# Sums of squares in four quarters of the array, and a square root taken by sides

## The chip, the core and the metric

The kernel runs on one core of a Trainium2 chip. The metric is the device time of one execution in microseconds (us); the median of the runs stands for a kernel. Engines are named as in the profile: PE (TensorE, matrix products), PEld (its weight loads), DVE (VectorE), ACT (ScalarE), POOL (GpSimd) and SP (SyncE, which here issues DMAs).

## The reference, cut to what matters

Four layers follow one another on a 48-channel image of 128 x 128: an attention over all pixels, sweeps along rows and columns, a convolution with 8 x 8 patches, and a state-space scan. Only the beginning of the first is edited:

```python
qkv = jnp.einsum('bchw,oc->bohw', x, qkv_w)
qkv = jax.lax.conv_general_dilated(qkv, dw_w, window_strides=(1, 1), padding='SAME',
                                   feature_group_count=3 * c, ...)
q, k, v = jnp.split(qkv, 3, axis=1)
...
def _l2norm(t, eps=1e-12):
    n = jnp.sqrt(jnp.sum(t * t, axis=-1, keepdims=True))
    return t / jnp.maximum(n, eps)
q = _l2norm(q)
k = _l2norm(k)
attn = jax.nn.softmax(jnp.einsum('bnc,bmc->bnm', q, k) * temperature, axis=-1)
```

Each pixel is a token with 48 channels of q, k and v. The token's q and its k are divided by their lengths, so the kernel needs, for every token, a sum of squares over the 48 channels of q and another over those of k.

## The kernel before, in words

`tile_kernel` (L1779) runs `attention`, `sweeps`, `patch_conv`, `scan_stats` and `scan` one after the other. `attention` (L121) has a first stage, which makes q, k and v, and then `attend` (L424), which does the softmax.

The first stage goes over 8 bands of 16 image rows, and each band has two *takes* of 8 rows, t0 to t15; a take is 1024 tokens, as two halves of CH = 512. Everything is fp32.

- `band(b)` (L237) fills one of two band buffers and one of two `rest` buffers: DVE writes normalised rows (L94), then 15 DMAs on SP's queue copy shifted rows (L265, L268 and twelve at L277) for the convolution. Band b+1 is filled while band b is worked on.
- `conv` (L280) does the 1x1 and 3x3 convolution as products on PE. `p[0]` and `p[1]` (one per half, a PSUM bank each) hold q and k: the 48 channels of q with their padding on partitions 0 to 63, those of k on 64 to 127. `pv` holds v of both halves, one on partitions 0 to 63, one on 64 to 127. The last products, `pv<-rest`, have 48 rows and 64 columns each: the first in rows 0 to 47 and columns 0 to 63 of the array, the second in rows 64 to 111 and columns 64 to 127.
- `take` (L319) squares `p[0]` and `p[1]` on ACT into `sq`, copies `pv` to `vt` on ACT, and sums the squares over the channels with one 128x128 product per half: `blk` is block diagonal, with ones in its two blocks of 48 x 64. So the result `pss[n]` has on partitions 0 to 63, in every row, the sum over q, and on 64 to 127 that over k. ACT takes the square root into `nrm`. PE then transposes `vt` into `pt`.
- `scale` (L346), on DVE: reciprocal of `nrm` (`rn`), and `f` = `p` times `rn`. DVE also copies `pt` into `v` (L378), after which POOL sets a part of `v` to one (L379).
- `split` (L353) of take k is issued after take k+1: ACT rounds `f` into the first part of `hl`, POOL subtracts for the second (L362), and per half four DMAs on SP carry `hl` off to `qm` and `keys` (L363 to L366). There are two `hl` buffers, one per half, so the casts of take k wait for the DMAs of take k-1.
- `moving(0)` (L162) loads the first queries back, with 12 DMAs on SP. It is issued in band 4, ahead of the DMAs of band 5.

The order on ACT and PE is that of the program (`InOrder`). The queues of all engines, SP's too, run in order: an instruction that waits holds up those behind it. A take on ACT is: two squares, `vt`, two roots, then the two casts of the split of the take before. In the last take the two `p` are copied to `late`, which frees their banks for `attend`.

`patch_conv` holds another place that matters below: its products `f<-qkv,fm` are four 64x64 products with 384 columns, one in each quarter of the array, written to two banks, one for the upper row half and one for the lower. Its source line in the profile, like that of all recorded engines, is L49.

Of the kernel before, what the change touches and what calls it, by code (L numbers as in the profile page):

```python
# [22 lines left out]
AF = mybir.ActivationFunctionType  # L23
# [97 lines left out]
def attention(ctx, tc, x1, mp, const, ins):  # L121
# [4 lines left out]
    ident, blk = const["ident"], const["blk"]  # L126
# [6 lines left out]
    for i in range(HALF // PART):  # L133
        t = images.tile([128, PART], F32, name=f"x{i}")
        nc.gpsimd.memset(t[32:64], 0.0)
        for half in range(2):
            at = half * HALF + i * PART
# [39 lines left out]
    with ExitStack() as a:  # L177
        act, pe = InOrder(tc, nc.scalar), InOrder(tc, nc.tensor)
# [140 lines left out]
        def take(t0, p, pv):  # L319

            sqs, psss, nrms = [], [], []
            for n in range(2):
                sqs.append(sp.tile([128, CH], F32, name="sq"))
                act.activation(sqs[n], p[n], AF.Square)
            vt = once.tile([128, CH], F32, name="vt")
            act.copy(vt, pv)

            for n in range(2):
                psss.append(ps2.tile([128, CH], F32, name="pss"))
                pe.matmul(psss[n], lhsT=blk, rhs=sqs[n], start=True, stop=True)  # L330
                nrms.append(rp.tile([128, CH], F32, name="nrm"))
                act.activation(nrms[n], psss[n], AF.Sqrt)
            if t0 == N - 2 * CH:

                for n in range(2):
                    act.copy(late[n], p[n])
                p = late
            pt = ps1.tile([128, 4, 2, 64], F32, name="pt")
            for i in range(4):
                pe.transpose(  # L340
                    pt[:, i].rearrange("t n c -> t (n c)"), vt[:, i * 128 : (i + 1) * 128], ident
                )
            tv = slice(t0 // 128, t0 // 128 + 8)
            own = {}

            def scale(get):  # L346
                for n in range(2):
                    rn = rnp.tile([128, CH], F32, name="rn")
                    nc.vector.reciprocal(rn, nrms[n])
                    own[n] = get("f", n)  # L350
                    nc.vector.scalar_tensor_tensor(own[n], rn, 1e12, p[n], ALU.min, ALU.mult)

            def split(act, get):  # L353

                r, at = divmod(t0, N // 4)
                r *= 32
                for n in range(2):
                    f, hl = own[n], get("hl", n)
                    to = slice(t0 + n * CH, t0 + (n + 1) * CH)
                    kc = slice(at + n * CH, at + (n + 1) * CH)  # L360
                    act.copy(hl[:, 0].bitcast(F32R), f)
                    nc.gpsimd.tensor_sub(hl[:, 1].bitcast(F32R), f, hl[:, 0])  # L362
                    nc.sync.dma_start(parts_of[:, :, to], hl[0:C])  # L363
                    nc.sync.dma_start(keys[r : r + 32, 0:2, kc].bitcast(F32), hl[64:96])
                    for i in range(2):
                        nc.sync.dma_start(  # L366
                            keys[r + 16 * i : r + 16 * i + 16, 2, kc].bitcast(F32),
                            hl[96 : 64 + C, i],
                        )

            def get(name, n):
                if name == "hl":
                    return hlp.tile([128, 2, CH], F32, name=name)
                return fp.tile([128, CH], F32, name=name)

            if p is not late:
                scale(get)
            nc.vector.tensor_copy(v[:, tv, :].rearrange("t (n i) c -> t i n c", n=2), pt)  # L378
            nc.gpsimd.memset(v[:, tv, C:64], 1.0)  # L379
            return scale, split, get  # L380
# [3 lines left out]
        for b in range(NB):  # L384
            if b == NB // 2:
                first = moving(0)
            nxt = band(b + 1) if b + 1 < NB else None
            for y in range(0, R, 8):
                p = [ps.tile([128, CH], F32, name="p") for _ in range(2)]
                pv = ps1.tile([128, CH], F32, name="pv")  # L390
                t0 = (b * R + y) * W
                conv(p, pv, cur, y)
                more = take(t0, p, pv)
                if last:
                    last[1](act, last[2])
                last = more
            cur = nxt
# [1604 lines left out]
```

## Time and profile before

| what | us |
|---|---|
| median of 3 runs (lowest to highest) | 7003.15 (6998.90 to 7007.36) |
| the profiled execution | 7006.47 |
| its span, first to last instruction | 7004.7 |
| PE busy | 5671.9 (81% of the span) |
| ACT busy | 4517.3 (64%) |
| DVE busy | 4462.8 (64%) |
| POOL busy | 2825.9 (40%) |

The takes lie between 43 and 247 us of the span, `attend` from there to 3380 us. The busy shares are averages over stages with different bounds; a stage is read by its own rows, and by what ends last in it. In the profile a product of fp32 shows as two matrix passes, so two products count as x4. "rn", "pss" and so on are the tiles' names without buffer numbers, and `128*64 128x512` is the size of the weights, and that of the moving operand.

### The profile page before, as it was taken

The numbers are of one execution on the slowest core, as the hardware profiler recorded it, in microseconds if no ns is written. First come the engines' busy times: TensorE is split into PE (matmuls) and PEld (weight loads), VectorE is DVE, ScalarE is ACT, GpSimd is POOL, SyncE is SP. The second block draws the span as 40 slices with busy tenths as digits, with TensorE's granted clock in tenths as the row PEclk, the third lists the DMA queues.
The fourth block names the chain that finished last, engine by engine and source line by source line (L and its number), as shares of the span: only waits on it lengthen the run. The fifth ranks groups of instructions, "written<-read, shape, count | busy, mean of one in ns | idle before, by whom it ended". The sixth has DMA issues, their size and how long they took to land.

```text
span 7004.7 us, 217413 instructions
## 1 busy us (share of the span) xinstructions
PE 5671.9 (81%) x97896; PEld 3328.3 (48%) x97896; DVE 4462.8 (64%) x4604; ACT 4517.3 (64%) x6731; POOL 2825.9 (40%) x623
## 2 busy tenths in 40 slices
PE   8999999999999999999999996555455545555555
PEld 3444444444444444444677653444443434344444
DVE  6444434444344443444445445999999999999998
ACT  2677777777777777777440134766666666666665
POOL 2100000000000000000102223999999999999998
PEclk9999999999999999999999997777666767776666
DMA  5200000000000000000100112565566656566665
GB/s 101 65 11 16 16 17 12 15 16 16 17 11 17 16 16 17 11 16 10 34 21 3 46 23 63 161 165 165 161 160 159 164 159 162 155 166 167 182 177 147
DMA packets 214187, 534.76 MB, mean 76 GB/s; under 512 B 44419, under 2 KB 76210, under 8 KB 211346
## 3 DMA queue, kind: packets, MB, share of 16 engines
q1 hardware_dynamic: 201623, 511.07, 27.5%
q8 instruction: 769, 12.60, 0.8%
q10 hardware_dynamic: 11627, 9.71, 0.6%
q14 instruction: 168, 1.38, 0.1%
HBM read 464.51 MB, written 28.31 MB: 70 GB/s over the span
## 4 chain that ended last, share of the span: by engine, by line
PE 60%; DVE 25%; issue 6%; POOL 4%; ACT 2%; DMA 2%; SPq 1%; ACTq 0%; DVEq 0%; POOLq 0%
PE s L49 45%; DVE h L1754 22%; PE p L49 7%; PE y L49 3%; POOL h L49 3%; PE pp L49 1%; DVE xb L49 1%; PE pc L49 1%; ACT dA L49 1%; PE pv L49 1%; PE po L49 1%; DMA du<-rep 1%; DVE y L49 0%; ACT L49 0%; POOL y L1148 0%
## 5 line engine op out<-in xcount | busy, mean ns | idle before, releaser
L49 POOL TENSOR_TENSOR h<-du,bt 128x3072 f32<-128x3072 f32 (+1 forms) x386 | 2560.1, 6674 | 100.0 <-DMA du<-rep 56.0
L49 ACT ACTIVATE x<-s,temp 128x512 f32<-128x512 f32 x3076 | 1832.3, 693 | 677.7 <-PE s L49 677.7
L1754 DVE TENSOR_TENSOR_SCAN h<-dA,carry,h 128x1024 f32<-128x1024 f32 x864 | 1939.8, 2324 | 34.4 <-ACT dA L49 30.8
L49 PE MATMUL s<-x,v 128*64 128x512 f32 x8192 | 1870.5, 598 | 0.0
L49 ACT ACTIVATE dA<-dt,a 128x1024 f32<-128x1024 f32 x1152 | 1287.3, 1118 | 853.9 <-DVE h L1754 843.2
L49 PE MATMUL y<-h,cw 128*32 128x48 f32 x49152 | 908.0, 247 | 929.4 <-issue 478.6
L49 PE MATMUL s<-mq,keys 32*128 32x512 f32 x20480 | 1337.7, 401 | 2.4 <-ACT late L49 1.3
L49 PEld LDWEIGHTS y<-h,cw 128*32 128x32 f32 x49152 | 817.2, 141 | 1050.3 <-issue 626.6
L819 POOL MEMSET xb<- 128x256 f32 (+1 forms) x2 | 0.8, 412 | 3116.2 <-DVE end L49 3116.2
L49 PEld LDWEIGHTS s<-mq,keys 32*128 32x128 f32 x20480 | 952.5, 183 | 578.6 <-issue 415.2
L49 DVE TENSOR_TENSOR both<-s,both 128x512 f32<-128x512 f32 x480 | 331.9, 691 | 1350.6 <-PE s L49 1350.6
L49 PEld LDWEIGHTS s<-x,v 128*64 128x64 f32 x8192 | 542.8, 136 | 1064.6 <-issue 877.8
L49 DVE COPY x<-s 128x512 f32<-128x512 f32 x1020 | 704.0, 690 | 418.0 <-PE s L49 406.6
L49 ACT ACTIVATE x<-x,temp 128x512 f32<-128x512 f32 x1020 | 693.2, 749 | 0.0
L1754 DVE TENSOR_TENSOR_SCAN h<-dA,h 128x1024 f32<-128x1024 f32 x288 | 635.3, 2269 | 36.0 <-ACT dA L49 26.4
L49 PE MATMUL yz<-ev,sel 128*8 128x48 f32 x4096 | 192.5, 260 | 266.4 <-ACT ev L49 265.0
L49 PEld LDWEIGHTS yz<-ev,sel 128*8 128x8 f32 x4096 | 162.2, 106 | 324.7 <-ACT ev L49 296.2
L49 PE MATMUL p<-xb,l_w 112*48 112x78 f32 (+8 forms) x6096 | 227.3, 223 | 18.7 <-DVE xb L49 7.4
L49 PE MATMUL p<-xa,l_w 112*48 112x78 f32 (+8 forms) x6096 | 227.5, 224 | 15.1 <-DVE xa L49 6.0
L49 PEld LDWEIGHTS p<-xb,l_w 112*48 112x48 f32 x6096 | 193.4, 123 | 52.6 <-DVE xb L49 36.3
L49 PEld LDWEIGHTS p<-xa,l_w 112*48 112x48 f32 x6096 | 193.9, 123 | 48.7 <-DVE xa L49 30.5
L941 POOL TENSOR_TENSOR xb<-xb,xa 48x2048 f32<-48x2048 f32 (+2 forms) x10 | 45.1, 4506 | 402.4 <-DVE xa L49 371.5
(210 smaller groups left out, 3422.8 us busy)
## 6 DMA issues: line engine op xcount, KB each, us to landing
du<-rep SPq DMA_DIRECT2D x768, 256.0 KB
dt<-rep SPq DMA_DIRECT2D x768, 256.0 KB
mq<-qm SPq DMA_DIRECT2D x128, 128.0 KB
mq<-qm SPq DMA_DIRECT2D x256, 64.0 KB
qm<-hl SPq DMA_DIRECT2D x30, 192.0 KB
rep<-dd SPq DMA_DIRECT2D x24, 192.0 KB
yd<-ys ACTq DMA_DIRECT2D x256, 12.0 KB
keys<-hl SPq DMA_DIRECT2D x30, 128.0 KB
```

What stands on the lines that cost most here:

```text
L49: ins = method(*args, **kwargs).ins
L819: nc.gpsimd.memset(b[:, lines, pad], 0.0)
L941: nc.gpsimd.tensor_add(xr, xr, u[0:C, x : x + xr.shape[2], E : E + H].rearrange("c w h -> c h w"),)
L1754: nc.vector.tensor_tensor_scan(h[:, p, k, :], dA, h[:, p, k, :], carry[:, i, k : k + 1] if ci else 0.0, ALU.mult, ALU.add,)
```

## The change

The one product per half becomes two products of 64 rows and 64 columns, one for q's squares and one for k's. For the first half they lie in the two diagonal quarters of the array; for the second half in the other two, so that q's sums land on partitions 64 to 127 of `pss[1]` and k's on 0 to 63. All four are issued before the first square root. The root of the first half stays one activation; that of the second half becomes two, one for each side, which put the sides back.

```diff
+            sides = [slice(0, 64), slice(64, 128)]
             for n in range(2):
                 psss.append(ps2.tile([128, CH], F32, name="pss"))
-                pe.matmul(psss[n], lhsT=blk, rhs=sqs[n], start=True, stop=True)
+                for side in range(2):
+                    at = sides[side]
+                    pe.matmul(
+                        psss[n][sides[side ^ n]],
+                        lhsT=blk[at, at],
+                        rhs=sqs[n][at],
+                        start=True,
+                        stop=True,
+                    )
+            for n in range(2):
                 nrms.append(rp.tile([128, CH], F32, name="nrm"))
-                act.activation(nrms[n], psss[n], AF.Sqrt)
+                if n == 0:
+                    act.activation(nrms[n], psss[n], AF.Sqrt)
+                    continue
+                for side in range(2):
+                    act.activation(nrms[n][sides[side]], psss[n][sides[1 - side]], AF.Sqrt)
```

## The prediction

> **What bounds the kernel now.** I read the stretches by stage first, to see which engine fills the stage that is edited (columns: stretch, its length, then busy time and count of PE, PEld, DVE, ACT, POOL, granted clock, DMA share, GB/s).
>
> ```profile
> 43.00:247.00 204.00, 201.27 (x640) 75.32 (x640) 140.78 (x93) 61.88 (x110) 38.62 (x45) 0.98 0.46 98
> 247.00:3380.00 3133.00, 3131.45 (x28650) 1493.59 (x28652) 1269.89 (x1818) 2454.78 (x4099) 5.22 (x5) 1.00 0.05 15
> ```
>
> The sixteen takes (8 rows of the image each, t0 to t15) fill 43 to 247 us and TensorE is busy in 201 of 204. The attention after them is filled by TensorE too, so an earlier end of the takes moves everything behind it. A busy PE says little by itself; the chain of waits, cut to this stage, says it is the bound (start, length, what).
>
> ```profile
> 70.39 6.21 PE p L49 x16
> ...
> 177.19 1.98 DMA keys<-hl
> ...
> 180.57 3.00 PE pss L49 x4
> ```
>
> One take repeats every 12.29 us (p starts at 57.93, 70.22, 82.52, 94.81 in the timeline). Once, before t10's products, the chain leaves PE and runs through SP's queue and a DMA. The stage so has two bounds: PE, and at one place SP.
>
> Then PE's timeline, around one take's products and in the later patch stage:
>
> ```profile
> 66.96 1.07 PE L49 MATMUL pv<-rest,wt 48*64 48x512 f32 x4
> 67.97 1.98 PE L49 MATMUL pss<-sq,blk 128*128 128x512 f32 x4
> 68.50 0.19 PEld L49 LDWEIGHTS pss<-sq,blk 128*128 128x128 f32 x1 [0.24 <-issue]
> 68.93 0.19 PEld L49 LDWEIGHTS pss<-sq,blk 128*128 128x128 f32 x1 [0.24 <-issue]
> 69.79 0.60 PE L49 MATMUL pt<-ident,vt 128*128 128x128 f32 x4
> ...
> 3944.31 0.88 PE L49 MATMUL f<-qkv,fm 64*64 64x384 f32 x8
> 3945.11 0.87 PE L49 MATMUL po<-k,gm 128*64 128x384 f32 x4
> ```
>
> Each product is two passes (x4 for two products), 0.43 apart, one behind the other: from 67.97 to 69.79, 1.82 us. `f` is the row that decides: four 64x64 products in the four quarters, eight passes of 384 columns, done in 0.80. A 384-column pass is 0.43 x 384/512 = 0.32; two are 0.64, four would be 1.29. So four quarters do run abreast here. `pv<-rest` has two diagonal quarters: four passes in 1.01, not 1.72.
>
> **The change part by part.** *Products.* Removed per take: four full passes, 1.72. Added: eight quarter passes, four abreast, 0.86. The first pass after a change of tile size costs about 0.1 more than 0.43 (67.97 to 68.50 is 0.53), and the load ahead of it can't be prefetched (about 0.1). Before, that falls between `pv<-rest` (64-wide quarters) and pss (whole array); after, pss has the quarters of `pv<-rest` and the switch falls between pss and the transposes. One switch either way. Start of `pv<-rest` to the next take's p: now 70.22 - 66.96 = 3.26; then 0.91 + 0.96 + 0.53 = 2.40. Saved 0.86 per take. The transposes also wait for vt on ACT (68.17 + 0.58 = 68.75); they would start at 68.83, so it just fits (0.05 a take if it doesn't).
>
> Here a rule of the Trainium skill speaks against the change: TensorEngine Tiling, Restrictions and Gotchas, Gotcha 1, says that different row tiles cannot access one PSUM bank simultaneously. In `f` each row half has its own bank; in the new code each pss bank is written by both row halves. By the rule the first product's two quarters go one behind the other, and so do the second's; in order of issue only the middle two of the four overlap: six passes, 2.6 us, 0.86 more per take instead of less. But `pv<-rest` is two row halves into the one bank of pv, and takes 1.01, as `p<-rest` does with two banks (63.18 to 64.24, 1.06). The row contradicts the rule for two quarters; no row shows it for four. I take abreast (sum -10.3), and keep the rule (sum +11) for the rivals.
>
> *Square roots.* The second is split: one activation more per take, 0.49 from start to start (245.75 to 246.24 below), whether on 64 or 128 partitions (the copy on 64x512 is 578 ns, that on 128x512 585). 16 x 0.49 = 7.8 us on ACT, which is busy 62 of 204. The 5 us ACT waits for PE's p in most takes cover it. Without that cover it would cost 0.49 a take; that happens once, at the end.
>
> ```profile
> 245.75 0.60 ACT L49 ACTIVATE nrm<-pss 128x512 f32<-128x512 f32 x1 [0.26 <-PE pss L49]
> 246.24 1.07 ACT L49 COPY late<-p 128x512 f32<-128x512 f32 x2
> ```
>
> t15's copies `late` release the banks of the attention. After: products done at 244.65, roots at 244.70, 245.18, 245.66, `late` at 246.15 instead of 246.24. t15 gains 0.1, not 0.86. Reading PSUM partitions 64 to 127 into 0 to 63 on ACT is not in the trace; DVE does it in `second`. I take no cost.
>
> *Order.* No DVE or POOL instruction changes place; PE and ACT only have the new ones. On SP one 16-row DMA to `keys` of t0's split comes two places earlier, ahead of one to `qm` and one to `keys`; it needs less than these, and SP is idle there until 72.47: nothing. The product that waits for the second square is now the third; that square is done at 65.48, over 2 us before (t10 apart, below).
>
> *What is late next.* DVE needs 2 x (3.35 + 0.68) + 0.63 + about 1 = 9.7 per take; PE's new period is 11.43, so it stays ahead. SP does not:
>
> ```profile
> 153.86 0.58 SPq L168 DMA_DIRECT2D mq<-qm  x1
> ...
> 159.68 0.52 SPq L265 DMA_DIRECT2D band<-band  x1
> 160.25 3.41 SPq L268 DMA_DIRECT2D band<-band  x2
> 163.71 8.64 SPq L277 DMA_DIRECT2D rest<-band  x12
> ...
> 176.56 1.22 SPq L366 DMA_DIRECT2D keys<-hl  x2
> ```
>
> Band 5 and t7's split stand behind the 12 DMAs of `moving(0)` (5.8 us). t8's casts to hl on ACT wait for t7's buffers (until 179.40), and t10's squares wait behind those casts: pss of t10 starts at 180.57, 1.9 late. From band 3 (104.73) to 177.78 SP has only two real gaps: 2.8 before t4's split (124.40) and 2.1 before t6's (148.99). Both end with POOL's subtraction, queued behind a memset that follows the copy of the take's pt; so their ends come with PE. A take's first root comes 0.2 earlier within the take. Band 3 itself so comes 3 x 0.86 + 0.2 = 2.8 earlier (t2's split before it hangs on t3's copy), t4's split 5 x 0.86 + 0.2 = 4.5, t6's 7 x 0.86 + 0.2 = 6.2. Each gap loses 1.7 and is left with 1.1 and 0.4; from t6's split on SP is dense, nothing more can be won, and t10's squares come 6.2 earlier. PE gets there 10 x 0.86 + 0.1 = 8.7 earlier. So 2.5 of the gain turns into stall: 1.9 becomes 4.4.
>
> The Trainium skill (TensorE: Matmul & The Clock Gate, Part 1) has the clock halved after an idle window of about 3.4 us. In the trace 1.9 idle was enough: granted clock 0.50 from 182 to 184, and pss to p took 3.64 instead of 2.26, a loss of 1.4. By the rule the longer stall costs one window at half, 1.7. I take 1.5, as now; none would give 1.2 more, two windows 1.7 less.
>
> Sum: up to t10's pss 6.2; that block itself 0.6 (two passes saved, but the second pair waits 0.5 for the second square); t11 to t14 4 x 0.86 = 3.4; t15 0.1. Together 10.3. The profiled execution took 7006.5 (span 7004.7, 1.8 around it) and would take 6996.2; it stands 3.3 above the median, within 6998.9 to 7007.4. From the median: 7003.15 - 10.3 = 6992.9.
>
> **The rivals.** *Less stall.* If SP issues some 4% quicker (`rest` in 7.8, not 8.6) and the clock stays up, 13; without any stall 15 x 0.86 + 0.1 + 3.4 = 16.4: 6987 to 6990. For it: the other bands' take 7.7 to 7.8, one 8.5. Against: SP is dense, and 5% slower over the 100 us of its dense stretch it gives back 5: 6998.
>
> *Two abreast.* Two quarters, then two: four passes again, PE as now, 0.5 more on ACT at the end: 7003.5. Against it, `f`.
>
> *The bank serialises (slower).* Place: the pss block. Price: the rule's six passes, +0.86 a take, 13.8, less some 3 of the stall it hides: +11, 7014; all eight one behind another, 3.43 instead of 1.72, 27.4 - 3 = +24, 7027. It decides from a block over 1.82 us. For it: four abreast in shared banks is in no row. Against: `pv<-rest`.
>
> **How the numbers follow.** A measurement of this kernel can tell about 0.2%, 14 us, from no change. As drawn up, 0.53, of which a tenth reads beyond 14; less stall 0.25, most of it beyond 14 once the scatter of 4 either way is added; two abreast 0.10; serialised 0.12, mostly over. Faster 0.27, same 0.62, slower 0.11. The likeliest's own range, 6989 to 6998, is the clock's (-1.2 to +1.7), SP's 5, and the scatter of 4. The range that holds 8 in 10 takes in less stall with its scatter and two abreast, and leaves out the serialised case: 6984 to 7004.
>
> **What would show it.** pss as x8 with 64*64, `pv<-rest` to pss 0.91, pss to pt 0.96; p every 11.43; t10's pss at about 174.4 after 4.4 idle behind `sq`; ACT's late copies near 236. A pss block of 1.8 or more, a take not shorter than 12.29, or transposes waiting for vt by more than 0.1 would prove it wrong; t10 without a longer stall would move it to 6988.

## The result, and the profile after

| | before | after |
|---|---|---|
| median of 22 runs each (lowest to highest) | 7002.97 (6996.47 to 7010.94) | 6993.90 (6984.93 to 6996.71) |
| the profiled execution | 7006.47 | 6985.35 |
| its span | 7004.7 | 6983.5 |
| first p of t1 to the attention's first product | 57.93 to 247.41 = 189.48 | 54.36 to 234.57 = 180.21 |

The ratio is 0.9985 with a 95% interval of 0.9979 to 0.9991: 9.1 us less, a small gain, within the 0.2% that was called no change. 6992.9 was forecast.

The two profiled executions differ by 21 us, and that is not the size of the change. From t1's first p to the attention the difference is 9.3; t0, which that stretch leaves out, saves another 0.9. So 10.2 come from the edited stage. The rest lies outside it: t0's products started 1.6 earlier in this execution (41.22 against 42.86), its p then took 1.0 less (7.07 against 8.09), as the granted clock left 0.50 sooner, and the stages from the attention's first product on were some 8 shorter. A second execution of the same kernel (the seventh experiment) took as long as before for those later stages (6757.5 from the attention's first product to the end of the span, before 6757.3), so these 8 are scatter and not the change.

The stage in the stretches (stretch, its length, busy time and count of PE, PEld, DVE, ACT, POOL, granted clock, DMA share, GB/s):

```profile
43.00:237.00 194.00, 187.97 (x735) 69.70 (x737) 144.68 (x96) 74.33 (x129) 40.71 (x47) 0.98 0.48 103
237.00:3370.00 3133.00, 3131.95 (x28646) 1470.90 (x28642) 1268.60 (x1818) 2455.80 (x4101) 3.13 (x3) 1.00 0.06 15
```

PE is still what fills it, with 188 of 194; ACT went from 62 to 74, of which 16 more roots are some 10; the attention is as it was. The chain of waits of this execution does not reach back into the takes (its first piece is at 234.47), so a take's order is read from PE's timeline (start, length, what):

```profile
63.39 0.65 PE L49 MATMUL pv<-rest,wt 48*64 48x512 f32 x2
63.42 0.65 PE L49 MATMUL pss<-sq,blk 64*64 64x512 f32 x2
63.87 0.60 PE L49 MATMUL pv<-rest,wt 48*64 48x512 f32 x2
63.90 1.43 PE L49 MATMUL pss<-sq,blk 64*64 64x512 f32 x6
65.26 0.66 PE L49 MATMUL pt<-ident,vt 128*128 128x128 f32 x4
65.75 5.32 PE L49 MATMUL p<-band,wt 128*128 128x512 f32 x12
...
159.31 7.09 PE L49 MATMUL p<-band,wt 128*128 128x512 f32 x12 [2.28 <-DMA band<-band]
170.11 1.08 PE L49 MATMUL pv<-rest,wt 48*64 48x512 f32 x4
172.48 1.56 PE L49 MATMUL pss<-sq,blk 64*64 64x512 f32 x8 [1.29 <-ACT sq L49]
174.46 5.32 PE L49 MATMUL p<-band,wt 128*128 128x512 f32 x12
...
218.93 1.20 PE L49 MATMUL pss<-sq,blk 64*64 64x512 f32 x8
220.06 0.65 PE L49 MATMUL pt<-ident,vt 128*128 128x128 f32 x4
```

The first six lines are one take. From `pv<-rest` to the transposes it takes 1.87, where 0.91 + 0.96 was forecast; one p follows another every 11.39 (before 12.29, forecast 11.43). But the four quarters do not start together: two passes of pss start 0.03 after `pv<-rest`, beside it. The middle lines are t10 with its stall, now two waits (2.28 and 1.29), neither of which is the 4.4 that was forecast. The last two, in t14, are the four quarters abreast in two banks: eight passes in 1.13, where two by two they would need four times 0.43. From `pv<-rest` (218.19) to the transposes this take needs the same 1.87; why it goes the other way is open.

ACT's timeline, around one take's roots and at the end of the stage:

```profile
64.59 0.58 ACT L49 COPY vt<-pv 128x512 f32<-128x512 f32 x1 [2.68 <-PE pss L49]
65.38 1.81 ACT L49 ACTIVATE nrm<-pss 128x512 f32<-128x512 f32 x3 [0.20 <-PE pss L49]
...
231.57 1.81 ACT L49 ACTIVATE nrm<-pss 128x512 f32<-128x512 f32 x3 [0.22 <-PE pss L49]
233.39 1.07 ACT L49 COPY late<-p 128x512 f32<-128x512 f32 x2
```

By the order of the program the first half's two products are issued first. Yet the first half's root waits 0.20 and starts at 65.38, when the *last* passes are done (the row of six ends at 63.90 + 1.43 = 65.33). So the pair that ran beside `pv<-rest` isn't the first half's, though that is issued first: it is the second half's, in the quarters that `pv<-rest` leaves free. And three roots take 1.81; with 0.60 for one, that is 0.605 from one to the next and not 0.49. Reading the other side's partitions cost nothing that shows: a root by sides took 0.591, and one on its own side (experiment 6) as long.

### The profile page after: what moved, and what is told of

Same layout as the page of the kernel before. It is cut to its first block, busy times and chain, and to the rows that moved or that the text cites. A ratio compares the mean times of both kernels' runs of the same rounds, so it can differ in the third digit from the quotient of the medians.

```text
span 6983.5 us, 217558 instructions
## 1 busy us (share of the span) xinstructions
PE 5650.6 (81%) x97960; PEld 3297.6 (47%) x97960; DVE 4464.2 (64%) x4604; ACT 4528.4 (65%) x6747; POOL 2826.0 (40%) x623
## 4 chain that ended last, share of the span: by engine, by line
PE 56%; DVE 25%; issue 6%; POOL 4%; ACT 2%; DMA 1%; SPq 0%; ACTq 0%; DVEq 0%; POOLq 0%
PE s L49 45%; DVE h L1768 23%; PE p L49 6%; POOL h L49 3%; PE y L49 3%; PE pp L49 1%; PE pc L49 1%; DVE xb L49 1%; ACT dA L49 1%; PE po L49 1%; DMA du<-rep 1%; DVE y L49 1%; ACT L49 0%; POOL y L1162 0%; POOL y L1163 0%
## 5 line engine op out<-in xcount | busy, mean ns | idle before, releaser
L49 PEld LDWEIGHTS s<-mq,keys 32*128 32x128 f32 x20480 | 930.2, 183 | 599.2 <-issue 415.6
L49 PE MATMUL p<-xa,l_w 112*48 112x78 f32 (+7 forms) x6096 | 228.7, 224 | 14.9 <-DVE xa L49 5.9
```

The lines of the kernel that those rows point to most:

```text
L49: ins = method(*args, **kwargs).ins
```

## The experiments

Each is compared with the kernel before on its own chip. "Stage" is the time from t1's first p to the attention's first product. "Lost" is what the takes from t1 to t15 took beyond 14 times their ordinary period.

| kernel | ratio (95% interval) | period | lost | stage |
|---|---|---|---|---|
| before | 1 | 12.29 | 3.6 | 189.5 |
| after | 0.9985 (0.9979 to 0.9991) | 11.39 | 6.7 | 180.2 |
| 1 both halves on the diagonal | 0.9997 (0.9988 to 1.0006) | 12.25 | 2.0 | 187.0 |
| 2 both off the diagonal | 0.9993 (0.9984 to 1.0002) | 11.40 | 7.5 | 181.6 |
| 3 after, queries loaded in band 7 | 0.9980 (0.9971 to 0.9989) | 11.39 | 0 | 173.5 |
| 4 before, queries loaded in band 7 | 0.9997 (0.9988 to 1.0006) | 12.29 | 0 | 185.8 |
| 5 halves swapped, queries in band 7 | 0.9976 (0.9966 to 0.9987) | 11.39 | 0 | 173.3 |
| 7 after once more | 0.9981 (0.9972 to 0.9990) | 11.39 | 8.1 | 181.6 |
| 8 halves swapped | 0.9981 (0.9972 to 0.9990) | 11.39 | 8.7 | 181.8 |
| 9 as 5, once more | 0.9975 (0.9966 to 0.9985) | 11.39 | 0 | 173.2 |

The theory after the first result: the gain comes from the quarters that `pv<-rest` leaves free; a part of it is lost, at t10 above all, to SP's queue. The rivals: smaller products are quicker wherever they lie; the four run abreast and that is the gain; the stall at t10 has nothing to do with SP's order.

**1, both halves on the diagonal.** The products keep their new size and lie where `pv<-rest` lies; both roots stay whole.

```diff
-                        psss[n][sides[side ^ n]],
+                        psss[n][sides[side]],
```

> Both halves' products in the two diagonal quarters, each root one activation again (128 partitions). Two theories of where the 0.9 us per take comes from. Free quarters: it comes from the pair in the off-diagonal quarters, which runs beside pv<-rest (itself on the diagonal); without such a pair the passes queue up behind pv<-rest as two and two: start of pv<-rest to pt 2.73 us instead of 1.87, a take 12.25 to 12.29 apart, time that of the kernel before (ratio 0.9995 to 1.0005). Smaller products: it comes from products of 64x64 being cheaper in themselves: 1.87 as in the changed kernel, ratio 0.9985.

Its timeline of PE:

```profile
88.25 1.08 PE L49 MATMUL pv<-rest,wt 48*64 48x512 f32 x4
89.16 1.88 PE L49 MATMUL pss<-sq,blk 64*64 64x512 f32 x8
90.98 0.66 PE L49 MATMUL pt<-ident,vt 128*128 128x128 f32 x4
```

No pss pass starts until `pv<-rest` is through, and the eight passes take 1.82, two by two: what the four full ones took. The median is 6996.56 against 6996.84 before. So neither the product's size nor its instruction count gains anything; of 0.90 per take, 0.86 are gone. It also shows the "two abreast" rival at its price. Its stage is 2.5 shorter than before all the same: 0.6 is the takes' 0.04, and most of the rest is that the clock was not halved at t10 in this execution.

**2, both halves off the diagonal.** All four products now lie in the two free quarters, and both roots go by sides.

```diff
-                        psss[n][sides[side ^ n]],
+                        psss[n][sides[1 - side]],
...
-                if n == 0:
-                    act.activation(nrms[n], psss[n], AF.Sqrt)
-                    continue
```

> Both halves' products in the two off-diagonal quarters, so both roots are taken by sides (four activations per take). Free quarters: the first pair runs beside pv<-rest, the second after it: four slots of 0.43, start of pv<-rest to pt 1.87 us, a take 11.4 apart, ratio 0.9985 to 0.999 (0.5 more on ACT at the end). Four abreast (what the prediction reckoned with): the gain needs the two pairs in different quarters; here they share two, so the block is two slots for pv<-rest and four for pss, 2.73 us, a take 12.25, ratio 1.000.

Its timeline of PE:

```profile
89.45 0.65 PE L49 MATMUL pv<-rest,wt 48*64 48x512 f32 x2
89.46 0.65 PE L49 MATMUL pss<-sq,blk 64*64 64x512 f32 x2
89.93 0.60 PE L49 MATMUL pv<-rest,wt 48*64 48x512 f32 x2
89.94 1.45 PE L49 MATMUL pss<-sq,blk 64*64 64x512 f32 x6
91.33 0.66 PE L49 MATMUL pt<-ident,vt 128*128 128x128 f32 x4
```

1.88 from `pv<-rest` to the transposes, as with the change, although the two halves share their quarters here: the last six passes take 1.45, two by two. Half of the sums lie under `pv<-rest`, the other half behind it. That settles the cause: it is the two free quarters beside `pv<-rest`, and four abreast isn't needed. The trace settles it, not the time: the median is 5.0 lower (6991.82 against 6996.84), a ratio of 0.9993 where 0.9985 to 0.999 was expected, and its interval takes in no change; 7.5 were lost at t10. The arithmetic of the forecast came out because both ways need as many slots of 0.43: before, six (two for `pv<-rest`, four for the full passes); after, four. In the forecast the last two hold four pss passes each; in the trace each of the four holds two.

**3, the first queries loaded later.** The changed kernel with the 12 DMAs of `moving(0)` issued in band 7 instead of band 4, out of the way of band 5.

```diff
-            if b == NB // 2:
+            if b == NB - 1:
```

> The changed kernel with moving(0) issued in band 7 instead of band 4, so that band 5's DMAs don't stand behind its 12 DMAs on SP. Queue theory: t10 starts at once after t9 (no 2.3 us for band 5), its squares are not late (no 1.3 us), and the clock is not halved (1.8 us): the takes end some 4 to 5 us earlier, 0.9980 against the kernel before, about 6989. Rival: SP is dense to the end of band 5 whatever it carries, and the wait moves to a later take or to t13's split before the attention: less than 1 us, 0.9985.

Its chain of waits (start, length, what) now runs through all the takes, on PE alone up to the last roots:

```profile
155.87 0.86 PE pss L49 x6
157.31 6.21 PE p L49 x16
163.53 3.30 PE pv L49 x14
...
225.74 0.59 ACT nrm L49
226.94 1.08 ACT late L49 x2
228.12 1.82 PE s L49 x20
```

t10 (p at 157.31) waits for nothing. The stage is 6.7 shorter than with the change alone, more than the 4 to 5 expected: in the first profile of the changed kernel SP's queue cost 6.7. The median is 13.7 lower than before (6983.10 against 6996.84).

**4, the same in the kernel before.** The same edit, without the new products.

> The kernel before, with moving(0) issued in band 7 instead of band 4. Queue theory: the one stall of the takes, 1.9 us at t10 and 1.4 of halved clock, goes: 3.3 us, ratio 0.9995, and t10's pss starts at 178.7 of the span instead of 180.6. Rival: nothing, 1.000.

Takes of 12.29 throughout and a stage 3.6 shorter; its time (6995.64 against 6996.84) can't tell that from nothing. With 3 it gives the full worth of the change where the queue doesn't take any: 185.84 - 173.48 = 12.4, and 0.9 for t0. The medians of the two differ by 12.5.

**5, the halves swapped.** On 3, the first half goes off the diagonal and its root by sides, the second half on the diagonal with one root.

```diff
-                        psss[n][sides[side ^ n]],
+                        psss[n][sides[side ^ (1 - n)]],
...
-                if n == 0:
+                if n == 1:
```

> As e3_after_mq7, and the halves change places: the first half's products in the off-diagonal quarters (its root taken by sides), the second half's on the diagonal (one root). If the off-diagonal pair does run beside pv<-rest, the first half's sums are there one pair (0.86 us) before the second's, so its two roots run before the second pair ends, and t15's copies late come 0.3 to 0.5 earlier than in e3 (12.4 after t15's p instead of 12.84); takes 11.39 apart as there; ratio 0.998. If instead the pairs go in the order of issue, the diagonal pair is never first here and nothing changes: 12.84.

Its timeline of ACT in t15, whose p starts at 213.97:

```profile
224.17 0.59 ACT L49 COPY vt<-pv 128x512 f32<-128x512 f32 x1 [2.66 <-PE pss L49]
224.78 1.82 ACT L49 ACTIVATE nrm<-pss 64x512 f32<-64x512 f32 x3
226.50 1.07 ACT L49 COPY late<-p 128x512 f32<-128x512 f32 x2
```

The first half's root no longer waits: it follows `vt` at once. So the off-diagonal pair is the early one in either order of issue. From p to the late copies it is 12.53 instead of 12.84.

**6, the split root alone.** The kernel before, with the second root taken as two, each on its own side; a single run.

```diff
-                act.activation(nrms[n], psss[n], AF.Sqrt)
+                if n == 0:
+                    act.activation(nrms[n], psss[n], AF.Sqrt)
+                    continue
+                for side in range(2):
+                    at = slice(64 * side, 64 * side + 64)
+                    act.activation(nrms[n][at], psss[n][at], AF.Sqrt)
```

> The kernel before, with the second half's root alone split in two (64 partitions each, no change of sides), products as before. Cover theory: hidden in t0 to t14, takes 12.29 apart as before; in t15 the copies late come 0.5 to 0.6 later after t15's p (13.1 instead of 12.55). Rival, ACT as the bound: the casts of every split are later and the takes are stretched by 0.1 or more each. One time, near 7003 within the scatter.

Its timeline of ACT in t15, whose p starts at 230.69:

```profile
241.89 0.60 ACT L49 ACTIVATE nrm<-pss 128x512 f32<-128x512 f32 x1 [0.41 <-PE pss L49]
242.75 1.19 ACT L49 ACTIVATE nrm<-pss 64x512 f32<-64x512 f32 x2 [0.26 <-PE pss L49]
243.95 1.07 ACT L49 COPY late<-p 128x512 f32<-128x512 f32 x2
```

Takes stay at 12.29, so the extra root is hidden in every take but the last. There the late copies come 13.26 after p instead of 12.55: 0.7 later, where 0.5 to 0.6 was expected. Two half roots take 1.20 up to the copy behind them, where one whole root took 0.49. The single time, 6997.30 beside a median of 6998.67 before, says nothing either way.

**7, 8 and 9, side by side.** The changed kernel again; the swap of 5 without the later load; and 5 again.

> The changed kernel once more, beside the two below on one chip. From t1's first p to the first attention product the profile should give 180.2 again (before: 189.5), with t10 waiting twice: for band 5's DMA, then for its squares, 3.6 together. If the 21 us between the two first profiles were the change's, the median would be some 20 below before's; by the takes alone it is 10 below (ratio 0.9985).

> The halves swapped and nothing else: the first half's products in the off-diagonal quarters with a root by sides, the second half's on the diagonal with one root; the first queries still load in band 4. Free-quarters theory: takes 11.39 apart as after. Root-spacing theory: t15 from p to the late copies 12.53 instead of 12.84, as in the run with both edits, so 0.3 less in all; t10 waits 3.6 as after. If the earlier end of t15 came from the later load of the queries, it is 12.84 here. Ratio to before 0.9985.

> The swapped halves with the first queries loaded in band 7, once more, to stand beside the changed kernel on one chip. From t1's first p to the attention 173.3 again, 6.9 less than the changed kernel's 180.2: ratio to before 0.9975, and its median 7 below that of the changed kernel. If the two queue-free profiles were only lucky, the medians lie within 3.

Medians against 7001.72 before: 6991.14, 6990.04 and 6983.73. The 20 below that the two first profiles would have meant did not come, the 10 below did. The stage of 180.2 and the 3.6 of waits expected for the seventh and eighth did not come again: the stages are 181.6 and 181.8, the waits 1.74 + 2.93 and 2.22 + 3.18. t15 is 12.54 from p to the late copies in the swap alone, so that belongs to the swap; 0.3 is too little for the median to show. The ninth lies 7.4 below the seventh, with 6.9 expected from the takes. Its ratio's interval and that of the seventh overlap, but the fifth, the ninth and the third experiment all have the stage near 173.

The seventh also shows the stall in another form. Its timeline of PE at t10 and t11:

```profile
158.90 5.39 PE L49 MATMUL p<-band,wt 128*128 128x512 f32 x12 [1.74 <-DMA band<-band]
172.00 2.46 PE L49 MATMUL pss<-sq,blk 64*64 64x512 f32 x8 [2.93 <-ACT sq L49]
175.30 6.54 PE L49 MATMUL p<-band,wt 128*128 128x512 f32 x12
```

And its stretches there (columns as above; the clock is third from the end):

```profile
172.00:174.00 2.00, 2.00 (x8) 0.58 (x8) 0.00 (x0) 0.92 (x2) 0.80 (x1) 0.50 0.49 129
...
176.00:178.00 2.00, 2.00 (x4) 0.85 (x3) 2.00 (x2) 1.10 (x2) 1.27 (x1) 0.56 1.15 187
```

Here the first wait is shorter (1.74), and the clock stays up in t10's p (5.39); the second is longer (2.93) and the clock is halved through the products of t10 (3.30 from pss to p instead of 1.98) and the first of t11 (6.54 instead of 5.32). In the first profile it was the other way round: halved between 161 and 164, in t10's p.

## Why the prediction was right, and where it was not

**The products, 0.86 a take: right in size, wrong in how.** Measured 0.90. The slots were counted rightly (four instead of six), but the four quarters hardly ever start together. PE starts a product whose quarter is free ahead of one that was issued earlier and has to wait (63.42 against 64.30). So the description of the kernel before, in which every engine's queue runs in order, does not hold for the starts of PE's products. Experiments 1 and 2 show where the gain comes from: none with the same quarters as `pv<-rest`, all of it with the others. The forecast's picture, four abreast behind `pv<-rest`, is what t14 shows, in the same 1.87. It isn't what the gain needs: by it experiment 2, with two quarters for all four products, would have gained nothing.

**The bank rule.** That two row halves cannot write one bank at the same time (the Trainium skill, TensorEngine Tiling (Array Packing), Restrictions and Gotchas) did not hold for four quarters either: 1.13 for the eight passes of t14, where the rule's six slots of 0.43 would be 2.6. The slower rival fell with that: at full clock no pss block took longer than the 1.82 of before, and outside the stall and its half clock no take was longer than 12.29.

**The transposes and vt: fits, as said.** `vt` ends at 65.17 and the transposes start at 65.26, 1.87 after `pv<-rest`, which is the forecast's own offset.

**The stall: right in place and nearly in size, wrong in form.** "1.9 becomes 4.4" behind the squares: measured 2.28 for band 5's DMA and 1.29 for the squares in one execution, 1.74 and 2.93 in the other. Two steps failed. The first is that only the squares hang on SP's queue. Band 5 stands in that queue too, and t10's p needs it first. SP's issue of these rows comes 3.4 earlier than before, counted from t1's p, and PE's demand 8.1 earlier (nine takes at 0.90); before, the DMA issues had ended 4.9 ahead of t10's p (160.25 + 3.41 against 168.58), now 2.7 (153.24 + 3.39 against 159.31), and PE waits.

The second is that SP's gaps shrink with PE, to 0.4 before t6's split. POOL's, ACT's and SP's timelines there, first before, then after:

```profile
147.48 0.20 POOL L379 MEMSET v<- 128x128 f32 x1 [10.82 <-DVE v L378]
147.69 2.61 POOL L362 TENSOR_TENSOR hl<-f,hl 128x512 fp32r<-128x512 f32 x2
148.99 0.31 SPq L363 DMA_DIRECT2D qm<-hl  x1
...
138.80 1.24 SPq L380 DMA_DIRECT2D keys<-hl  x2
139.02 0.62 ACT L49 CAST hl<-f 128x512 fp32r<-128x512 f32 x1 [3.49 <-DMA keys<-hl]
141.01 0.31 SPq L377 DMA_DIRECT2D qm<-hl  x1
...
145.89 0.58 SPq L168 DMA_DIRECT2D mq<-qm  x1
...
152.68 0.52 SPq L265 DMA_DIRECT2D band<-band  x1
153.24 3.39 SPq L268 DMA_DIRECT2D band<-band  x2
156.68 7.77 SPq L277 DMA_DIRECT2D rest<-band  x12
```

Before, POOL's subtraction for t6's split came behind the memset, and so behind PE. Now the memset is early (138.30), and the subtraction (139.72) waits for ACT's cast, which waits for a DMA of t5's split to free `hl`. So SP waits for its own earlier DMA, and the gap stays at 1.0 (in experiments 7 and 8 too). Counted from t1's p, t6's split comes 4.4 earlier than before and t10's squares 4.5, where the forecast's 6.2 is 5.3 without t0's take. SP's 12 `rest` DMAs took 7.77 instead of 8.64, as the "less stall" rival supposed; it brought no less stall, because `moving(0)` took 1.0 longer (145.89 to 152.68, before 153.86 to 159.68).

t12 lost another 0.5 (11.92 from its p to the next), which the forecast has nowhere: its squares stood behind a cast that waited for a DMA behind band 6's.

```profile
194.62 0.62 ACT L49 CAST hl<-f 128x512 fp32r<-128x512 f32 x1 [2.23 <-DMA keys<-hl]
195.14 1.07 ACT L49 ACTIVATE sq<-p 128x512 f32<-128x512 f32 x2
```

**The clock, 1.5 as now: between the two ends.** In the first profile the half clock fell into t10's p (7.09 instead of 5.32) and cost nothing further, since the squares came late anyway; in the seventh experiment it cost 2.5 over t10 and t11, against 1.4 plus 0.3 before. That, with the waits and t12's 0.5, is why the loss of the takes rose from 3.6 to 6.7 in the first profile, and to 8.1 in the seventh experiment: 3.1 and 4.5 more, where 2.5 was forecast for the stall.

**The roots, 0.49 each: too small.** t15 was to gain 0.1 and lost 0.3 (12.55 to 12.84 from p to the late copies). The spacing was read from a root and a copy behind it; between these roots, and from the last of them to the copy, it is 0.605, which makes 0.35 of the 0.4 that were missed. Otherwise they are hidden, as said.

The sum, part by part against the forecast's own terms (t0's 0.9 is in the first):

| gain, us | forecast | first profile | experiment 7 |
|---|---|---|---|
| up to t10's pss | 6.2 | 5.4 | 6.0 |
| from there to t11's p | 0.6 | 1.7 | 0.3 |
| t11 to t14 | 3.4 | 3.4 | 2.7 |
| t15 to the attention | 0.1 | -0.3 | -0.3 |
| together | 10.3 | 10.2 | 8.8 |

The medians say 9.1 and, in experiment 7, 10.6. The size of the gain per take was worked out, and it held. That the whole came within 0.1 of the first profile was luck: SP brought t10's squares 0.8 less early than forecast and the end lost 0.4, and the clock, which happened to be halved elsewhere, gave 1.1 back.

## What to carry to other kernels

Ask which quarters of the array the neighbouring products leave free, and put small products there: it is the place that gains, not the smaller size. When a bound engine gets faster, list everything in the other queue that it will reach sooner, each with its own slack, not only the wait that shows now: here 12 DMAs issued elsewhere took 6.7 more off a stage from which the change alone had taken 9.3. Judge a gain of 0.1% from the stage's own stretch in the profile, since two executions of one kernel differ by as much elsewhere (spans of 6983.5 and 6993.6 here).

## What the hardware showed that was not expected

- PE lets a later product start ahead of an earlier one if its quarters are free: 0.03 after `pv<-rest`, 0.88 ahead of the pair that the program issues before it (63.42 and 64.30).
- In the changed kernel a root on 64 partitions costs as much as one on 128 (591 and 597 ns), and the next instruction starts 0.60 after it, without the overlap of 0.1 that the copy behind a whole root has (0.49 before; 0.50 again in experiment 5, where the whole root comes last). Why is open.
- The length of an idle time of PE doesn't alone decide whether the clock is halved. At t10 it was halved after 1.79 (experiment 6), 1.88 (before) and 2.28 (after); it was not after 1.76 (experiment 1), 1.86 (experiment 2) and 2.22 (experiment 8); after 2.93, 2.96 and 3.18 (experiments 7, 2 and 8) it was. So the same change's stall cost 2.5 more in one execution, and nothing in the other. What else decides is open.
